# The last map's gate products on two column tiles and its LoRA products on four row tiles of TensorE

## The chip, the cores and the metric

The kernel runs on one core of a Trainium2 chip. The metric is device time in microseconds (us), the median of several executions. One further execution was recorded by the profiler; all durations below come from that one.

## The reference, cut to what matters

The program is a two-layer decoder on two batch rows of 512 tokens and 1024 features, all in float32: a quantized product with the context, a linear map with LoRA, a cross attention with 32 heads, and a last map with LoRA. The change is in the last map (with one small part in the first linear map, which shares a helper). The last map is:

```python
def _L1_ffn_ref(x, W_up, gate_w, expert_bias, lora_A, lora_B):
    x_flat = x.reshape(-1, H)                                  # H = 1024, E = 4 experts, R = 8
    logits = x_flat @ gate_w.T + expert_bias
    top1 = jnp.argmax(logits, axis=-1)
    one_hot = jax.nn.one_hot(top1, E, dtype=x_flat.dtype)
    base_out = jnp.einsum('bth,oh->bto', x, W_up)
    z = jnp.einsum('nh,erh->ner', x_flat, lora_A)
    d = jnp.einsum('ner,ehr->neh', z, lora_B) * SCALE          # SCALE = 1
    delta = jnp.einsum('neh,ne->nh', d, one_hot)
    return base_out + delta.reshape(B, T, H)
...
x = x + _L1_ffn_ref(_layernorm(x, axis=-1), L1_ffn_W_up, L1_ffn_gate_w, L1_ffn_expert_bias, L1_ffn_lora_A, L1_ffn_lora_B)
```

So each token needs 36 numbers from its normalized row (4 logits and 4 x 8 values of z), keeps the 8 values of the expert with the largest logit, and adds a rank-32 product of them to its output row.

## The kernel before

**Stages.** In order of time: keys and values of both batch rows with the quantized product beside them, the first linear map (about 470 to 600 us of the span), the queries, 64 attention heads (two batch rows of 32) until about 2380 us, and the last map, woven into the end of the attention for batch row 0 and alone for batch row 1. Rows 0 to 3 of a batch row are its four tiles of 128 tokens; `rows(b, t)` is tile t.

**The big products.** Every 512 x 1024 x 1024 map is done as seven half-size products instead of eight (a Strassen-like scheme), by `seven_onto` (L304). A map is two blocks s = 0, 1, called a and b here; each does its products in the order 1, 2, 6, 7, 5, 4, 3. Each product is four matmuls over the contraction into one PSUM bank (`accumulate`, L345), taken by VectorE (L320, L317; ScalarE at L315 for product 1) into the rows. Products 1 and 6 give a common sum u, and GpSimd adds u to the outputs of products 5, 4 and 3, each time after VectorE has added that product (L322). `pair` (L325) interleaves them as a1 b1 a2 b2, then a's other five, then b's other five.

**The LoRA products before.** In `linear` (L562), products 2, 4, 5 and 3 of each block take a fifth matmul (L575 to L577): `tT()` holds the selected z of the tokens, transposed, with 32 used rows padded to 128, as halves of the tokens and their difference (`split_tokens`, L585), and `bl` is lora_B, padded to 128 rows. So one map has 8 LoRA matmuls.

**The gate before.** `gated` (L939) is a generator. Four steps multiply, for each tile t of 128 tokens, the normalized rows (as weights, 128 x 128) with the 36 gate and LoRA-A columns `ga_t` (as the moving operand) over 8 chunks of the contraction, into one wide PSUM tile (L946). A step on VectorE then selects the expert, tile by tile (L958 to L970, seven small instructions for each), into z, whose unused columns GpSimd has set to zero (L968). The last step transposes the four z on TensorE (L980), copies them out (L981) and takes the difference of the halves.

**Order.** TensorE runs its instructions in the order in which they are written, in the whole kernel. From the start of the attention's loop to the end of head 63's softmax, VectorE, ScalarE and GpSimd do so too; outside of it their order is a planner's. `hooks` (from L1174) hang pieces of the last map of batch row 0 onto phases of the attention's loop. After phase 1 of iteration 62 come the four gate steps (L1188), after phase 2 of that iteration the selection (L1189), after phase 1 of iteration 63 the transposes of z (L1207) and products a1 and b1 (L1213). In phase 2 of iteration 62, GpSimd gets the four sums of head 63's softmax (L801 to L806), and ScalarE the copy of that head's maximum (L791) and its exponentials (L798), which VectorE prepares (L795). Once the attention's loop has given the rest of its projection, products a4 to b3 of batch row 0 are woven with the layer norm, transposes (L204; copied out by ScalarE, L205, and VectorE, L206) and gate of batch row 1 by `turned_and_gated` (L1227); then the map of batch row 1 runs alone (L1247 to L1251), and its four rows are written out (L1253).

**Buffers.** PSUM has two wide buffers of two banks (`ps_wide`) and four of one bank (`ps_b`, and `ps_tr` of the same kind).

Of the kernel before, what the change touches and what calls it, by code (L numbers as in the profile page):

```python
# [39 lines left out]
def decoder_kernel(  # L40
# [263 lines left out]
    def seven_onto(product, place, order=(1, 6, 2, 7, 5, 4, 3)):  # L304

        banks = {}
        for i in order:
            first = {2: 1, 4: 7, 3: 5}.get(i, i)
            if i == first:
                banks[i] = ps_b()  # L310
            acc = banks[first]
            product(i, acc, i == first)
            if i == 1:
                u = u2([P, HALF])
                nc.scalar.copy(u, acc)  # L315
            elif i == 6:
                nc.vector.tensor_tensor(u, u, acc, ALU.add)  # L317
            else:
                c = place(*{2: (0, 0), 7: (1, 1), 5: (1, 1), 4: (1, 0), 3: (0, 1)}[i])
                nc.vector.tensor_tensor(c, c, acc, ALU.add)  # L320
                if i != 2 and i != 7:
                    nc.gpsimd.tensor_tensor(c, c, u, ALU.add)  # L322
            yield
# [238 lines left out]
    def linear(b, h_ops, w_ops, tT, bl):  # L562

        def blocks(s):
            lora = {2: (0, 0), 4: (1, 0), 5: (1, 1), 3: (2, 1)}

            def product(i, acc, start):
# [12 lines left out]
                (1, 2, 6, 7, 5, 4, 3),  # L580
            )
# [357 lines left out]
    def gated(quarters):  # L939


        zT, diff = u2([P, S]), u2([P, 256])
        gaccs = ps_wide().rearrange("p (t n) -> p t n", t=NT)
        for t in range(NT):
            for c in range(NC):
                nc.tensor.matmul(  # L946
                    gaccs[:, t, :NGA],
                    chunk(quarters, c, t),
                    ga_t[:, c, :],
                    start=(c == 0),  # L950
                    stop=(c == NC - 1),
                )
            yield
        zs = []
        for t in range(NT):
            gacc = gaccs[:, t, :]
            lg = small([P, E1])
            nc.vector.tensor_tensor(lg, gacc[:, :E1], eb_t, ALU.add)  # L958
            mx = small([P, 1])
            nc.vector.tensor_reduce(mx, lg, AX.X, ALU.max)  # L960

            nc.vector.tensor_scalar(lg, lg, mx, None, ALU.is_equal)
            nc.vector.tensor_tensor(lg, lg, prefer, ALU.mult)
            nc.vector.tensor_reduce(mx, lg, AX.X, ALU.max)
            nc.vector.tensor_scalar(lg, lg, mx, None, ALU.is_equal)
            if t % 2 == 0:
                z2 = u2([P, 2, P])
                nc.gpsimd.memset(z2, 0.0)  # L968
            z = z2[:, t % 2]
            nc.vector.tensor_tensor(  # L970
                z[:, : E1 * R1].rearrange("p (e r) -> p e r", r=R1),
                gacc[:, E1:NGA].rearrange("p (e r) -> p e r", r=R1),
                lg.unsqueeze(2).to_broadcast([P, E1, R1]),
                ALU.mult,
            )
            zs.append(z)
        yield
        tr = ps_tr()
        for t, z in enumerate(zs):
            nc.tensor.transpose(tr[:, t, :], z, ident)  # L980
        nc.vector.tensor_copy(zT, tr.rearrange("p t n -> p (t n)"))  # L981
        yield split_tokens(zT, diff)
# [193 lines left out]
    for i in range(2):  # L1176
# [11 lines left out]
    hooks[(62, 1)] = [lambda: advance(last["gates"], 4)]  # L1188
    hooks[(62, 2)] = [  # L1189
        lambda: next(last["gates"]),  # L1190
# [3 lines left out]
    with tc.manual_schedule(  # L1194
# [6 lines left out]
        for i in range(3 * (B * NH + 2)):  # L1201
# [4 lines left out]
            if (n - 2, phase) == (63, 1):  # L1206
                zTs = [next(last["gates"]), None]  # L1207
# [3 lines left out]
                nc.sync.dma_start(bl_t, bl1T)  # L1211
                main = linear(0, h_ops, w_ops, lambda: zTs[0], bl_t)
# [9 lines left out]
    for _ in steps:  # L1222
        pass
    hs, norms = normed(1, u4, 4)
    gates = gated(hs)

    def turned_and_gated():  # L1227
        next(norms)
        yield
        next(norms)  # L1230
        yield
        for _ in range(3):
# [3 lines left out]
        next(gates)  # L1236
        yield
# [9 lines left out]
    main = linear(1, token_sums(hs, lambda: u4([P, 4, 256])), w_ops, lambda: zTs[1], bl_t)  # L1247
    advance(main, 2)
    zTs[1] = next(gates)
    for _ in main:  # L1250
        pass  # L1251
    for t in range(NT):
        nc.sync.dma_start(out[1, ts(t, P), :], rows(1, t))  # L1253

# [70 lines left out]
```

## Time and profile before

| what | value |
|---|---|
| time, median of 3 executions | 2483.03 us (2481.97 to 2484.73) |
| the profiled execution: its own time | 2484.01 us |
| its span, first to last instruction | 2482.2 us |
| TensorE matmul, busy | 2436.6 us, 98% of the span |
| VectorE, ScalarE, GpSimd busy | 1839.0, 527.7, 1029.8 us |
| mean granted TensorE clock | 0.991 |
| L946 gate products, both batch rows | 128 recorded matmuls, 16.1 us |
| L347 (all products through `accumulate`) | 3648 recorded matmuls, 1410.8 us |

How to read it: a busy TensorE means that a matmul was in flight, not that the array was full. A float32 matmul of the program is recorded as two passes, each with a weight load (PEld) of its own: the 32 calls at L946 for one batch row stand as 64 records. In a timeline, a line has the start, the time from the first start to the last end, the engine with its line and operation, output and inputs with shapes, and how many instructions were merged; in brackets, how long the engine sat idle before it and who ended that. Matmul ends are modelled, so the start of the next group is the safer mark. PEclk is the granted TensorE clock as a share of full speed.

### The profile page before, as it was taken

To read this page: it belongs to the slowest core of one execution; us is meant where nothing else is said; L and a number is where in the kernel's file an instruction comes from. 1 tells how busy PE (TensorE), PEld (TensorE's weight loads), DVE (VectorE), ACT (ScalarE), POOL (GpSimd) and SP (SyncE) were. 2 spreads that over 40 slices of the span, in tenths; PEclk is the share of its full clock that TensorE was granted. 3 is DMA by queue.
4 is the path that set the end of the run, shared out by engine and by line. 5 is a ranking of instruction groups with operands and counts; after the bars stand their busy time and mean duration, and the time that the engine had idled before them with its cause. 6 is when DMAs were issued, how large, how long until landed. Compare 5 with 4: busy or idle time off the path is not lost.

```text
span 2482.2 us, 19693 instructions
## 1 busy us (share of the span) xinstructions
PE 2436.6 (98%) x6848; PEld 1216.4 (49%) x6856; DVE 1839.0 (74%) x2020; ACT 527.7 (21%) x615; POOL 1029.8 (41%) x552
## 2 busy tenths in 40 slices
PE   7999999999999999999999999999999999999999
PEld 3477458654444443444444444444444444445454
DVE  5848774345886546898888888888898888887552
ACT  1201221011222222322222222222222222222100
POOL 0000010111000002677676767676767576767421
PEclk8999999999999999999999999999999999999999
DMA  7225133013795221343323322542334234324301
GB/s 264 104 88 208 68 122 116 26 60 114 274 335 201 76 97 47 106 128 115 86 79 103 115 84 75 143 148 78 114 110 128 64 98 115 108 70 111 127 26 43
DMA packets 148243, 283.83 MB, mean 114 GB/s; under 512 B 29296, under 2 KB 47232, under 8 KB 146352
## 3 DMA queue, kind: packets, MB, share of 16 engines
q1 hardware_dynamic: 107888, 242.25, 29.0%
q10 hardware_dynamic: 39824, 39.60, 6.5%
q8 instruction: 55, 0.90, 0.1%
q0 software_dynamic: 432, 0.71, 0.1%
q14 instruction: 44, 0.36, 0.0%
HBM read 221.44 MB, written 61.08 MB: 114 GB/s over the span
## 4 chain that ended last, share of the span: by engine, by line
PE 73%; DVE 7%; POOL 2%; issue 2%; DMA 1%; ACT 1%; POOLq 0%; SPq 0%; ACTq 0%; DVEq 0%
PE b L347 38%; PE wide L749 16%; PE b L812 15%; PE wide L713 2%; DVE u L795 1%; PE wide L204 1%; DMA u<-in_wo_dram 1%; PE wide L946 1%; PE b L636 1%; DVE u L763 1%; POOL u L805 1%; DVE u L775 1%; DVE u L773 0%; POOL u L804 0%; DVE u L320 0%
## 5 line engine op out<-in xcount | busy, mean ns | idle before, releaser
L347 PE MATMUL b<-u,u 128*128 128x512 f32 (+1 forms) x3648 | 1410.8, 544 | 23.2 <-DVE u L291 10.2
L347 PEld LDWEIGHTS b<-u,u 128*128 128x128 f32 x3648 | 692.4, 191 | 706.8 <-issue 625.1
L812 PE MATMUL b<-u,u 128*128 128x512 f32 x1024 | 463.4, 596 | 0.0
L749 PE MATMUL wide<-u,u 128*128 128x512 f32 x1024 | 455.5, 596 | 7.1 <-DVE u L763 6.2
L763 DVE TENSOR_TENSOR u<-wide,u 128x1024 f32<-128x1024 f32 x256 | 313.0, 1225 | 135.7 <-PE wide L749 134.3
L798 ACT ACTIVATE u<-u 128x2048 f32<-128x2048 f32 x128 | 244.6, 1911 | 654.3 <-DVE u L795 572.3
L749 PEld LDWEIGHTS wide<-u,u 128*128 128x128 f32 x1024 | 194.1, 191 | 257.0 <-issue 178.2
L795 DVE TENSOR_TENSOR u<-u,b 128x2048 f32<-128x2048 f32 x128 | 290.2, 2269 | 0.0
L801 POOL TENSOR_TENSOR u<-u 128x1024 f32<-128x1024 f32 x64 | 151.5, 2367 | 318.8 <-ACT u L798 309.6
L812 PEld LDWEIGHTS b<-u,u 128*128 128x128 f32 x1024 | 187.5, 193 | 186.5 <-issue 186.5
L322 POOL TENSOR_TENSOR u<-u,u 128x512 f32<-128x512 f32 x120 | 189.2, 1597 | 197.5 <-DVE u L320 177.9
L320 DVE TENSOR_TENSOR u<-u,b 128x512 f32<-128x512 f32 x200 | 135.8, 680 | 135.4 <-PE b L347 135.3
L222 POOL TENSOR_TENSOR u<-u,sin_t 128x512 f32<-128x512 f32 x8 | 11.7, 1457 | 387.2 <-ACT u L217 387.2
L804 POOL TENSOR_TENSOR u<-u,u 128x1024 f32<-128x1024 f32 x64 | 150.6, 2354 | 36.1 <-ACT u L798 35.7
L805 POOL TENSOR_TENSOR u<-u,u 128x1024 f32<-128x1024 f32 x64 | 151.6, 2369 | 5.0
L823 POOL TENSOR_TENSOR u<-u,u 128x512 f32<-128x512 f32 x64 | 117.8, 1841 | 21.8 <-DMA u<-row 21.8
L1062 POOL DMA_DIRECT2D u<-in_b_dram x1 | 0.6, 558 | 303.5 <-DVE u L245 303.5
L216 ACT ACTIVATE u<-u 64x512 f32<-64x512 f32 x72 | 45.2, 628 | 350.1 <-DVE u L293 168.5
L713 PEld LDWEIGHTS wide<-ident,u 128*128 128x128 f32 x512 | 80.1, 204 | 65.8 <-issue 54.6
L771 DVE TENSOR_TENSOR u<-u 128x1024 f32<-128x1024 f32 x64 | 110.9, 1732 | 0.0
L773 DVE TENSOR_TENSOR u<-u,u 128x1024 f32<-128x1024 f32 x64 | 105.2, 1644 | 0.2
L806 POOL TENSOR_TENSOR u<-u 128x512 f32<-128x512 f32 x64 | 100.5, 1570 | 5.0
(127 smaller groups left out, 1648.3 us busy)
## 6 DMA issues: line engine op xcount, KB each, us to landing
u<-row ACTq DMA_DIRECT2D x128, 256.0 KB, 3.7
u<-wo SPq DMA_DIRECT2D x64, 512.0 KB, 4.2
u<-in_wo_dram SPq DMA_DIRECT2D x48, 512.0 KB, 4.5
u<-in_wq_dram SPq DMA_DIRECT2D x32, 512.0 KB, 4.0
q<-u SPq DMA_DIRECT2D x64, 256.0 KB, 2.4
u<-in_wo_dram SPq DMA_DIRECT2D x16, 1024.0 KB, 7.9
wo<-u SPq DMA_DIRECT2D x32, 512.0 KB, 4.7
u<-q SPq DMA_DIRECT2D x64, 256.0 KB, 4.5
```

The source lines that it names most:

```text
L320: nc.vector.tensor_tensor(c, c, acc, ALU.add)
L322: nc.gpsimd.tensor_tensor(c, c, u, ALU.add)
L347: nc.tensor.matmul(acc, lhsT, rhs, start=start and k == 0, stop=k == len(pairs) - 1, skip_group_check=True,)
L713: nc.tensor.transpose(tr[:, t, :], src[:, t, :], ident)
L749: nc.tensor.matmul(sc[:, ts(n, HALF)], self.kT[:, ts(2 * j + n, P)], self.qT, start=True, stop=True,)
L763: nc.vector.tensor_tensor(self.e[j // 2][:, js, :], sc.rearrange("p (k q) -> p k q", k=2), mask[j], ALU.add)
L795: nc.vector.tensor_tensor(e, e, self.nmf.unsqueeze(1).to_broadcast([P, 4, S]), ALU.add)
L798: nc.scalar.activation(e, e, AF.Exp)
L801: nc.gpsimd.tensor_tensor(d, e[:, 0:2, :], e[:, 2:4, :], ALU.add)
L804: nc.gpsimd.tensor_tensor(d, d, e[:, 0:2, :], ALU.add)
L805: nc.gpsimd.tensor_tensor(d, d, e[:, 2:4, :], ALU.add)
L812: nc.tensor.matmul(self.acc, self.v[:, k, :], self.e[j][:, k % 4, :], start=(k == 0), stop=(k == NKT - 1),)
```

## The change

The gate products of `gated` swap their operands. The 36 columns become the weights and the normalized rows move past them, 256 tokens at a time. Even chunks of the contraction go to the column tile of the array whose results land in PSUM partitions 0 to 35, odd chunks to the one for partitions 64 to 99, so two partial sums arise. ScalarE copies them into a tile `sums` that GpSimd has zeroed, TensorE transposes `sums` back to tokens in rows, and VectorE adds the two partial sums. The selection is done in one set of instructions for all four token tiles, and z is written four times, side by side, so that after its transpose every group of 32 partitions holds a copy.

The LoRA products leave `linear`. The new `add_lora` does them with a contraction of 32 on four row tiles, four matmuls for each pair of token tiles, each into a bank of its own, and VectorE adds the results to the rows. It is called once for each batch row: for row 0 after the attention's last projection, for row 1 after product b2. `bl_t` is loaded as four copies of the 32 used rows.

`seven_onto` gets an option that `linear` uses for both linear maps: GpSimd adds u to the three outputs as soon as product 6 has completed it. Finally, in the output of batch row 1, tile 1 is written last, in two halves.

```diff
--- before.py
+++ after.py
@@ -301,9 +301,14 @@
                 emit(0, 1, u)
             yield
 
-    def seven_onto(product, place, order=(1, 6, 2, 7, 5, 4, 3)):
+    def seven_onto(product, place, order=(1, 6, 2, 7, 5, 4, 3), u_first=False):
 
         banks = {}
+        places = {2: (0, 0), 7: (1, 1), 5: (1, 1), 4: (1, 0), 3: (0, 1)}
+
+        def add(c, what):
+            nc.gpsimd.tensor_tensor(c, c, what, ALU.add)
+
         for i in order:
             first = {2: 1, 4: 7, 3: 5}.get(i, i)
             if i == first:
@@ -315,11 +320,14 @@
                 nc.scalar.copy(u, acc)
             elif i == 6:
                 nc.vector.tensor_tensor(u, u, acc, ALU.add)
+                if u_first:
+                    for k in (5, 4, 3):
+                        add(place(*places[k]), u)
             else:
-                c = place(*{2: (0, 0), 7: (1, 1), 5: (1, 1), 4: (1, 0), 3: (0, 1)}[i])
+                c = place(*places[i])
                 nc.vector.tensor_tensor(c, c, acc, ALU.add)
-                if i != 2 and i != 7:
-                    nc.gpsimd.tensor_tensor(c, c, u, ALU.add)
+                if i != 2 and i != 7 and not u_first:
+                    add(c, u)
             yield
 
     def pair(a, b):
@@ -562,7 +570,7 @@
     def linear(b, h_ops, w_ops, tT, bl):
 
         def blocks(s):
-            lora = {2: (0, 0), 4: (1, 0), 5: (1, 1), 3: (2, 1)}
+            lora = {} if tT is None else {2: (0, 0), 4: (1, 0), 5: (1, 1), 3: (2, 1)}
 
             def product(i, acc, start):
                 pairs = [
@@ -578,6 +586,7 @@
                 product,
                 lambda i, j: rows(b, 2 * i + s)[:, ts(j, HALF)],
                 (1, 2, 6, 7, 5, 4, 3),
+                True,
             )
 
         return pair(blocks(0), blocks(1))
@@ -939,47 +948,71 @@
     def gated(quarters):
 
 
-        zT, diff = u2([P, S]), u2([P, 256])
-        gaccs = ps_wide().rearrange("p (t n) -> p t n", t=NT)
-        for t in range(NT):
+        zT = u2([P, S])
+        z = u2([P, NT, P])
+
+        acc, sums = ps_b(), u2([P, S])
+        nc.gpsimd.memset(sums, 0.0)
+        parts = [slice(64 * i, 64 * i + NGA) for i in range(2)]
+        for th in range(2):
             for c in range(NC):
                 nc.tensor.matmul(
-                    gaccs[:, t, :NGA],
-                    chunk(quarters, c, t),
+                    acc[parts[c % 2], ts(th, 256)],
                     ga_t[:, c, :],
-                    start=(c == 0),
-                    stop=(c == NC - 1),
+                    quarters[th][c // 4][:, c % 4, :],
+                    start=(c < 2),
+                    stop=(c >= NC - 2),
                 )
-            yield
-        zs = []
+            for part in parts:
+                nc.scalar.copy(sums[part, ts(th, 256)], acc[part, ts(th, 256)])
+            yield
+        tr, both = ps_tr(), u2([P, NT, NGA])
         for t in range(NT):
-            gacc = gaccs[:, t, :]
-            lg = small([P, E1])
-            nc.vector.tensor_tensor(lg, gacc[:, :E1], eb_t, ALU.add)
-            mx = small([P, 1])
-            nc.vector.tensor_reduce(mx, lg, AX.X, ALU.max)
-
-            nc.vector.tensor_scalar(lg, lg, mx, None, ALU.is_equal)
-            nc.vector.tensor_tensor(lg, lg, prefer, ALU.mult)
-            nc.vector.tensor_reduce(mx, lg, AX.X, ALU.max)
-            nc.vector.tensor_scalar(lg, lg, mx, None, ALU.is_equal)
-            if t % 2 == 0:
-                z2 = u2([P, 2, P])
-                nc.gpsimd.memset(z2, 0.0)
-            z = z2[:, t % 2]
+            nc.tensor.transpose(tr[:, t, :], sums[:, ts(t, P)], ident)
+        nc.vector.tensor_copy(both, tr[:, :, parts[0]])
+        nc.vector.tensor_tensor(both, both, tr[:, :, parts[1]], ALU.add)
+        lg = small([P, NT, E1])
+        by_expert = lambda t: t.unsqueeze(1).to_broadcast([P, NT, E1])
+        nc.vector.tensor_tensor(lg, both[:, :, :E1], by_expert(eb_t), ALU.add)
+        mx = small([P, NT])
+        by_token = mx.unsqueeze(2).to_broadcast([P, NT, E1])
+        nc.vector.tensor_reduce(mx, lg, AX.X, ALU.max)
+
+        nc.vector.tensor_tensor(lg, lg, by_token, ALU.is_equal)
+        nc.vector.tensor_tensor(lg, lg, by_expert(prefer), ALU.mult)
+        nc.vector.tensor_reduce(mx, lg, AX.X, ALU.max)
+        nc.vector.tensor_tensor(lg, lg, by_token, ALU.is_equal)
+        for k in range(4):
             nc.vector.tensor_tensor(
-                z[:, : E1 * R1].rearrange("p (e r) -> p e r", r=R1),
-                gacc[:, E1:NGA].rearrange("p (e r) -> p e r", r=R1),
-                lg.unsqueeze(2).to_broadcast([P, E1, R1]),
+                z[:, :, ts(k, E1 * R1)].rearrange("p t (e r) -> p t e r", r=R1),
+                both[:, :, E1:].rearrange("p t (e r) -> p t e r", r=R1),
+                lg.unsqueeze(3).to_broadcast([P, NT, E1, R1]),
                 ALU.mult,
             )
-            zs.append(z)
         yield
         tr = ps_tr()
-        for t, z in enumerate(zs):
-            nc.tensor.transpose(tr[:, t, :], z, ident)
+        for t in range(NT):
+            nc.tensor.transpose(tr[:, t, :], z[:, t, :], ident)
         nc.vector.tensor_copy(zT, tr.rearrange("p t n -> p (t n)"))
-        yield split_tokens(zT, diff)
+        yield zT
+
+    def add_lora(b, zT, bl):
+
+        K = E1 * R1
+        for i in range(2):
+            accs = [ps_wide() for _ in range(2)]
+            for k in range(4):
+                j, nh = k // 2, k % 2
+                nc.tensor.matmul(
+                    accs[j][:, ts(nh, HALF)],
+                    zT[ts(k, K), ts(2 * i + j, P)],
+                    bl[ts(k, K), ts(nh, HALF)],
+                    start=True,
+                    stop=True,
+                )
+            for j in range(2):
+                xs = rows(b, 2 * i + j)
+                nc.vector.tensor_tensor(xs, xs, accs[j], ALU.add)
 
 
     ctx.enter_context(tc.manual_schedule(engines={mybir.EngineType.PE}))
@@ -1185,9 +1218,8 @@
         fetch_rows,
         begin_map,
     ]
-    hooks[(62, 1)] = [lambda: advance(last["gates"], 4)]
+    hooks[(62, 1)] = [lambda: advance(last["gates"], 3)]
     hooks[(62, 2)] = [
-        lambda: next(last["gates"]),
         lambda: fetch_weight(7, 0, 1),
         lambda: fetch_weight(3, 1, 1),
     ]
@@ -1204,12 +1236,13 @@
             for act in hooks.get((n - 2, phase), ()):
                 act()
             if (n - 2, phase) == (63, 1):
-                zTs = [next(last["gates"]), None]
+                zT = next(last["gates"])
                 h_ops, parts = last["h"], last["w"]
                 w_ops = lambda i, c: parts[i - 1][:, c, :]
                 bl_t = u4([P, D])
-                nc.sync.dma_start(bl_t, bl1T)
-                main = linear(0, h_ops, w_ops, lambda: zTs[0], bl_t)
+                for k in range(4):
+                    nc.sync.dma_start(bl_t[ts(k, E1 * R1), :], bl1T[: E1 * R1, :])
+                main = linear(0, h_ops, w_ops, None, None)
                 advance(main, 2)
 
     h_ops[:] = token_sums(last["hs"], lambda: u4([P, 4, 256]))
@@ -1221,20 +1254,19 @@
     advance(main, 5)
     for _ in steps:
         pass
+    add_lora(0, zT, bl_t)
     hs, norms = normed(1, u4, 4)
     gates = gated(hs)
 
     def turned_and_gated():
         next(norms)
         yield
-        next(norms)
-        yield
-        for _ in range(3):
+        for _ in range(2):
+            next(norms)
+            yield
             next(norms)
             next(gates)
             yield
-        next(gates)
-        yield
         next(gates)
         yield
 
@@ -1244,13 +1276,18 @@
         pass
     for t in range(NT):
         nc.sync.dma_start(out[0, ts(t, P), :], rows(0, t))
-    main = linear(1, token_sums(hs, lambda: u4([P, 4, 256])), w_ops, lambda: zTs[1], bl_t)
+    main = linear(1, token_sums(hs, lambda: u4([P, 4, 256])), w_ops, None, None)
     advance(main, 2)
-    zTs[1] = next(gates)
+    zT = next(gates)
+    advance(main, 2)
+    add_lora(1, zT, bl_t)
     for _ in main:
         pass
-    for t in range(NT):
+
+    for t in (0, 2, 3):
         nc.sync.dma_start(out[1, ts(t, P), :], rows(1, t))
+    for i in range(2):
+        nc.sync.dma_start(out[1, ts(1, P), ts(i, HALF)], rows(1, 1)[:, ts(i, HALF)])
 
 
 def rope_tables():
```

## The prediction, made before the changed kernel was run

> **What bounds the kernel now.** I read the page's busy times first, then TensorE's timeline from 2240 us to the end, then the other engines at each gap in it. TensorE is busy 98% of the span, and in the first linear map every stretch of 10 us shows it busy for 10.00, so what counts is TensorE's time and the few places where it waits. This is TensorE alone around the gate of batch row 0, and then its last group:
>
> ```profile
> 2278.36 7.03 PE L347 MATMUL b<-u,u 128*128 128x512 f32 x16
> 2285.23 8.61 PE L946 MATMUL wide<-ga_t,u 128*128 128x36 f32 x64
> 2293.65 1.09 PE L713 MATMUL wide<-ident,u 128*128 128x128 f32 x4
> 2294.53 8.58 PE L812 MATMUL b<-u,u 128*128 128x512 f32 x16
> 2302.95 5.31 PE L347 MATMUL b<-u,u 128*128 128x512 f32 x12
> 2308.96 0.33 PE L980 MATMUL b<-ident,u 128*128 128x128 f32 x1 [0.70 <-DVE u L970]
> 2311.12 0.36 PE L980 MATMUL b<-ident,u 128*128 128x128 f32 x1 [1.83 <-DVE u L970]
> 2313.99 0.47 PE L980 MATMUL b<-ident,u 128*128 128x128 f32 x1 [0.93 <-DVE u L970]
> 2314.25 8.96 PE L347 MATMUL b<-u,u 128*128 128x512 f32 x16
> 2323.05 0.63 PE L713 MATMUL wide<-ident,u 128*128 128x128 f32 x4
> ...
> 2428.41 48.23 PE L347 MATMUL b<-u,u 128*128 128x512 f32 x112
> ```
>
> Sixteen passes of 512 columns take 6.87 us from start to start (2278.36 to 2285.23), 0.429 each. Sixteen at L812 took 8.42, and sixteen at L347 after the transposes 8.80. The windows by microsecond say why:
>
> ```profile
> 2291.00:2292.00 1.00, 1.00 (x7) 1.00 (x6) 0.00 (x0) 0.00 (x0) 1.00 (x2) 0.50 0.00 0
> 2312.00:2313.00 1.00, 0.42 (x1) 0.18 (x1) 0.82 (x5) 0.00 (x0) 0.00 (x0) 0.50 0.98 397
> ```
>
> After the window and the five engines, the last three numbers are clock, DMA share and GB/s: the clock halves twice, from about 2291 to 2297.3 in and after the gate products, and from 2311.7 to 2317.9 in and after the waits for z. Those waits come from VectorE's selection, which waits for GpSimd's zeroing:
>
> ```profile
> 2289.17 3.72 POOL L322 TENSOR_TENSOR u<-u,u 128x512 f32<-128x512 f32 x3
> 2299.88 2.36 POOL L801 TENSOR_TENSOR u<-u 128x1024 f32<-128x1024 f32 x1 [6.99 <-ACT u L798]
> 2308.37 0.56 POOL L968 MEMSET u<- 128x256 f32 x2
> ```
>
> The end is one product, VectorE's add, GpSimd's add and a DMA:
>
> ```profile
> 2476.68 0.69 DVE L320 TENSOR_TENSOR u<-u,b 128x512 f32<-128x512 f32 x1 [3.61 <-PE b L347]
> 2477.44 1.26 POOL L322 TENSOR_TENSOR u<-u,u 128x512 f32<-128x512 f32 x1 [3.03 <-DVE u L320]
> ```
>
> [...]idle from about 2308.3, half speed from 2311.7, full again 3.7 us after dense work began at 2314.25. [...] No tiled matmul is in this trace. [...]
>
> **1. Gate of batch row 0.** The old path, from L946 at 2285.2 to the transposes of head 63's sum (L713) at 2323.1, is 37.9 us. Now the new one. A pass of 256 columns takes 0.215 us (L636: 32 passes from 528.78 to 535.69). One half of the tokens is 8 matmuls, 16 passes, 3.43 us on one tile. If the two passes of one matmul follow each other on one tile, and passes start in order, the second pass of one tile can lie beside the first of the next: 8.5 slots, 1.83 us. Bounds: 1.72 (full overlap) to 3.43 (none). So the first half ends at 2287.0.
>
> Then ScalarE's copies need `sums` zeroed. That memset stands on GpSimd behind the three adds of the fence, which end at 2292.9; at twice 128x256 (0.31 us alone, 0.56 for two) it takes 0.5: 2293.4. Two copies of 36x256 follow. ScalarE takes 0.59 for 512 columns and 0.29 for one, hence 0.44 each: 2294.35. [...]TensorE waits until then, idle for 7.3 us and down to half clock: 3.4 us instead of 1.8, to 2297.8; two more copies, 2298.75; four transposes at 0.11, 2299.2. I assume that the clock is back then. Queued behind on TensorE are L713 (0.47) and L812 (6.87): 2306.6, where before they ended at 2302.95. So the first part loses 3.6 us.
>
> But z is then ready early. VectorE's selection is 12 instructions, two of 144 elements (0.25), six of 16 (0.16), four of 128 (0.3), with gaps 3.0 us in all: 2302.2. So the transposes of z at 2311.7 (after L347, 5.15) take 0.44 without a wait, the next 16 passes 6.87, and L713 stands at 2319.1 instead of 2323.1: **4.0 us won**. Behind the selection on VectorE stand L715, L786 and both L795; behind the copies on ScalarE L791. I followed them: VectorE's adds from 2303.2, exponentials until 2309.7, GpSimd's four sums until 2315.9. L713 of head 63 needs these, and 2315.9 is 3.2 us before 2319.1, so this cover holds; it is gone if GpSimd comes 3.2 us later. Bounds: no bank wait gives 6.2; no overlap of column tiles 2.4; a clock that doesn't recover in the second half takes another 2.1. I take 3.5.
>
> **2. LoRA of batch row 0.** Removed: 8 matmuls, 16 passes of 0.429, 6.86 us. Added: two groups of four row tiles. Each group is 8 passes; in order with one slot shared it takes 5 slots, 2.15 us[...]. VectorE's adds are 128x1024 out of PSUM, 1.23 us (L763's row). The second group needs the wide buffers that these adds free: the path is half a group, two adds, half a group. Here VectorE still has the last sum of weights (L267, 2.46, started at 2379.51 when a buffer came free) and two L320 ahead, so the first add begins about 2.1 us after the projection's end, the second group can use its buffers 3.3 and 4.6 after it, and ends at 5.9. In the old run TensorE stood 0.84 us here, waiting for L267; that is now covered. Net 6.86 - 5.9 + 0.84 = **1.8 won**; bounds 0.8 to 2.3.
>
> **3. Gate of batch row 1.** Removed: four groups of 16 passes at 0.107, 1.71 each, 6.84 us. Added: two halves of 1.83. Each now stands right behind the transposes of its own second token tile, which the old order had out of the way, and these copies take:
>
> ```profile
> 2396.10 0.59 ACT L205 COPY u<-wide 128x512 f32<-128x512 f32 x1 [3.72 <-PE wide L204]
> 2396.71 0.69 DVE L206 COPY u<-wide 128x512 f32<-128x512 f32 x1 [0.80 <-ACT u L205]
> ```
>
> The first four chunks need ScalarE's copy, so TensorE waits 0.65 in each half; VectorE's lands beside these four. Four transposes more, 0.44. Sum 2 x 2.48 + 0.44 = 5.4: **1.4 won**; without overlap 8.6, 1.8 lost. Memset and copies have 3.4 us of products beside them: nothing.
>
> **4. LoRA of batch row 1.** 6.86 removed. VectorE has one L320 (0.69) before: half a group 1.29, two adds 2.46, half a group 1.29, with handovers 5.2. **1.7 won**; bounds 0 to 2.6.
>
> **5. The end.** GpSimd's last add and its handover leave the path, 1.33 us. The last DMA is 256 KB instead of 512; the page has 2.4 us to landing for 256 KB (q) against 2.6 here, 0.2. **1.5 won**; bounds 1.2 to 1.9.
>
> **6. Mode changes.** About ten entries and exits. [...]a lone transpose with its latency is 0.33, so 0 to 0.33 each. I take 0.1: **1.0 lost**.
>
> **At nothing.** GpSimd's earlier adds in both linear maps: u is complete at product 6, the first add takes 1.26, and VectorE needs that output 3.43 later. The three extra DMA issues for `bl_t` (0.46 each on SP) delay wo loads that are used some 45 us later; the bytes are the same.
>
> Sum: 3.5 + 1.8 + 1.4 + 1.7 + 1.5 - 1.0 = 8.9. The profiled execution's own time is 2484.0 (span 2482.2 and 1.8 around it), so 2475.1; it stood 1.0 above the median, so **2474.0 us** for the median, 0.4% less.
>
> **The rivals.** **A: more overlap.** The second half doesn't wait for the copies, or all passes of different tiles lie side by side: 6.2 + 2.3 + 1.6 + 2.6 + 1.5 - 0.5 = 13.7, 2469. [...] **B: the tiles don't overlap** in float32: 2.4 + 0.8 - 1.8 + 0 + 1.5 - 1.0 = 1.9, 2481. What remains is the shorter end and the covered selection. **C: tiles that don't overlap[...].** There are some 24 changes for each batch row (16 in the gate, 8 in LoRA), 48 in all, in place of the 1.0. At half of a lone transpose, 0.165, they cost 7.9: 2.9 - 7.9, 5.0 lost, 2488. It decides for slower from 0.06 us a change. [...]
>
> **How the numbers follow.** Forecast 0.55 (2470.5 to 2478), A 0.22, B 0.18, C 0.05. A measurement of this kernel can tell 0.2%, 5 us, from no change, so faster is below 2478.1. That holds nearly all of the forecast, A, and a little of B: 0.77; same 0.18; slower 0.05. The range, 2468 to 2481, takes A's middle and B's, and leaves out C and the ends.
>
> **What would show it.** Gate: TensorE idle about 7 us between the halves, with half clock, and the memset at 2293; L980 without waits; L713 near 2319. LoRA: two groups with a wait for VectorE of about 0.5 to 1.3 in between. Starts in the tiled groups closer than a pass show overlap. End: no GpSimd after the last add. I am wrong if the passes don't overlap, if the clock stays low through L812, or if L713 of head 63 waits for GpSimd.

## The result, and the profile after

| what | before | after |
|---|---|---|
| time, median of 12 executions each | 2483.22 us (2480.85 to 2485.35) | 2475.72 us (2473.65 to 2482.5) |
| ratio after to before | | 0.9976, 95% interval 0.9968 to 0.9983 |
| the profiled execution: its own time | 2484.01 us | 2474.27 us |
| its span, and its mean granted clock | 2482.2 us, 0.991 | 2472.5 us, 0.992 |

The changed kernel is faster by 0.24%, about 6 us (4.2 to 7.9 by the interval). The forecast of 2474.0 was 1.7 us too low and its range holds the result; its gain of 9 us lies just outside the interval.

The two profiled executions differ by 9.7 us, but 4.3 of these lie ahead of the first changed instruction of the gate (it starts at 2285.23 before, at 2280.96 after), in stretches with the same instructions on TensorE. In the eight kernels below that have the changed kernel's TensorE code up to there, the gate starts anywhere from 2280.28 to 2285.60. So I count this part as chance and compare stage by stage from there:

| stretch of TensorE | before | after | won | forecast |
|---|---|---|---|---|
| gate of row 0 to the transposes of head 63's sum | 37.82 | 34.26 | 3.56 | 3.5 |
| from there to the first transposes of row 1 (L204) | 67.66 | 73.05 | -5.39 | -0.8 |
| from there to the transposes of z of row 1 | 37.26 | 33.57 | 3.69 | 4.0 |
| from there to the last matmul's end | 48.67 | 46.63 | 2.04 | 1.7 |
| from there to the span's end | 5.56 | 4.03 | 1.53 | 1.5 |
| sum | | | 5.43 | 9.9, less 1.0 for mode changes |

(In the forecast's column, the 1.8 of its step 2 is split: three of the eight removed products, 2.57, stood in the third stretch, so the second should have lost 0.8.) The 5.43 agree with the 6 of the ratio. One stretch is wrong, the second. TensorE's timeline of the kernel after, with its new line numbers (L959 gate, L971 transposes of the sums, L995 transposes of z, L722 and L821 what L713 and L812 were, L1006 the LoRA groups, L355 the products):

```profile
2280.96 1.93 PE L959 MATMUL b<-u,ga_t 128*36 128x256 f32 x16
2289.79 3.64 PE L959 MATMUL b<-u,ga_t 128*36 128x256 f32 x16 [6.91 <-ACT u L967]
...
2307.92 0.60 PE L995 MATMUL b<-ident,u 128*128 128x128 f32 x4
...
2315.22 0.63 PE L722 MATMUL wide<-ident,u 128*128 128x128 f32 x4
...
2370.72 1.14 PE L1006 MATMUL wide<-u,u 32*128 32x512 f32 x8
2373.95 2.08 PE L1006 MATMUL wide<-u,u 32*128 32x512 f32 x4 [2.09 <-DVE u L1015]
2376.65 2.07 PE L1006 MATMUL wide<-u,u 32*128 32x512 f32 x4 [0.61 <-DVE u L1015]
2378.65 9.79 PE L355 MATMUL b<-u,u 128*128 128x512 f32 x16
2388.27 1.03 PE L204 MATMUL wide<-ident,u 128*128 128x128 f32 x8
...
2431.68 2.26 PE L1006 MATMUL wide<-u,u 32*128 32x512 f32 x8 [1.31 <-DVE u L1015]
2433.87 34.60 PE L355 MATMUL b<-u,u 128*128 128x512 f32 x80
```

First the gate. Its 16 passes of 256 columns take 1.93 us, where one column tile takes 3.64 (measured below), so the column tiles overlap; then TensorE stands 6.91 us, the second half runs at half clock (3.64), and z is ready early enough that L995 has no wait. Then the LoRA groups of row 0. Eight passes take 1.14, where 8 x 0.429 = 3.43 is the estimate for one tile, so the row tiles overlap; but the second group waits 2.09 and 0.61, its halves of four passes take 2.08 each, and the 16 passes behind it 9.62 from start to start, not 6.87. Row 1 has the same wait shape, 1.31, and the 80 passes after it at full speed (34.60, 0.43 each). The windows of the kernel after (clock third from the right) show the cause of the 9.62:

```profile
2375.00:2376.00 1.00, 1.00 (x4) 0.00 (x0) 1.00 (x2) 0.00 (x0) 0.00 (x0) 0.50 0.00 0
...
2384.00:2385.00 1.00, 1.00 (x4) 0.52 (x3) 0.00 (x0) 0.00 (x0) 0.00 (x0) 0.99 0.00 0
```

In windows of 0.1 us the half clock lasts from 2373.8 to 2384.0. VectorE's timeline shows why the second group was late:

```profile
2372.69 1.21 DVE L1015 TENSOR_TENSOR u<-u,wide 128x1024 f32<-128x1024 f32 x1
2374.78 0.69 DVE L163 BATCH_NORM_STATS2 small<-u 128x6 f32<-128x512 f32 x1 [0.88 <-POOL u L310]
2375.39 1.20 DVE L1015 TENSOR_TENSOR u<-u,wide 128x1024 f32<-128x1024 f32 x1
```

The first add comes 2.0 us after the projection's end (2370.72), as forecast. Between it and the second stands an instruction of row 1's layer norm (L163), which itself waits 0.88 for GpSimd: TensorE can use the second buffer 5.9 us after the projection's end, 1.3 later than forecast. GpSimd's timeline at the gate, and the last line of the whole timeline:

```profile
2284.80 3.70 POOL L310 TENSOR_TENSOR u<-u,u 128x512 f32<-128x512 f32 x3
2288.43 0.53 POOL L955 MEMSET u<- 128x512 f32 x1
```

```profile
2469.30 0.33 SPq L1290 DMA_DIRECT2D out_dram<-u  x1
```

The zeroing stands behind three adds of the projection, and at the end no GpSimd add is left between VectorE's last add (2468.58 to 2469.27) and the last DMA's issue.

### The profile page after: what moved, and what is told of

Same layout as the page of the kernel before. It is cut to its first block, busy times and chain, and to the rows that moved or that the text cites. A ratio compares the mean times of both kernels' runs of the same rounds, so it can differ in the third digit from the quotient of the medians.

```text
span 2472.5 us, 19595 instructions
## 1 busy us (share of the span) xinstructions
PE 2422.1 (98%) x6800; PEld 1201.3 (49%) x6800; DVE 1839.4 (74%) x1994; ACT 530.4 (21%) x623; POOL 1031.2 (42%) x550
## 4 chain that ended last, share of the span: by engine, by line
PE 74%; DVE 6%; POOL 2%; issue 2%; DMA 1%; ACT 1%; ACTq 0%; SPq 0%; POOLq 0%; DVEq 0%
PE b L355 39%; PE wide L758 16%; PE b L821 15%; PE wide L722 2%; DVE u L804 2%; PE wide L204 1%; POOL u L814 1%; DVE u L772 1%; POOL u L813 1%; PE b L645 1%; DMA u<-in_wo_dram 1%; DVE u L782 1%; DVE u L784 1%; ACT u L807 0%; DVE u L328 0%
## 5 line engine op out<-in xcount | busy, mean ns | idle before, releaser
L355 PE MATMUL b<-u,u 128*128 128x512 f32 (+1 forms) x3616 | 1397.0, 544 | 22.5 <-DVE u L291 10.2
L355 PEld LDWEIGHTS b<-u,u 128*128 128x128 f32 x3616 | 687.2, 191 | 699.0 <-issue 615.8
L821 PE MATMUL b<-u,u 128*128 128x512 f32 x1024 | 460.4, 593 | 0.0
L821 PEld LDWEIGHTS b<-u,u 128*128 128x128 f32 x1024 | 186.4, 192 | 184.4 <-issue 184.4
L722 PEld LDWEIGHTS wide<-ident,u 128*128 128x128 f32 x512 | 80.1, 204 | 65.2 <-issue 55.1
```

Source lines behind the costliest of these rows:

```text
L355: nc.tensor.matmul(acc, lhsT, rhs, start=start and k == 0, stop=k == len(pairs) - 1, skip_group_check=True,)
L821: nc.tensor.matmul(self.acc, self.v[:, k, :], self.e[j][:, k % 4, :], start=(k == 0), stop=(k == NKT - 1),)
```

## The experiments

My theory after the comparison: the tiled products themselves are nearly free; what the change costs is two places in which TensorE waits inside a tiled sequence (the zeroing in the gate, VectorE's adds in the LoRA groups), and the half clock after each. Rivals: row tiles bring the clock down by themselves; the waits only move elsewhere. The first four kernels ran on one chip (before there: 2482.68), the next four on another (2482.62), the last three on a third (2483.74); each is compared by its ratio to the kernel before.

**The three parts alone.** Each kernel is the kernel before with one part of the diff: the gate (with z still padded and the LoRA products still in `linear`); the LoRA groups (with the old gate, z written four times for each token tile); `u_first` and the order of the output. Against the kernel before, beside the lines of the diff that each takes over, the first two have:

```diff
-        yield split_tokens(zT, diff)
+        yield split_tokens(zT, u2([P, 256]))
```

```diff
+            for k in range(4):
+                nc.vector.tensor_tensor(
+                    z[:, ts(k, E1 * R1)].rearrange("p (e r) -> p e r", r=R1),
...
-        yield split_tokens(zT, diff)
+        yield zT
```

and the third only takes over lines:

```diff
+    def seven_onto(product, place, order=(1, 6, 2, 7, 5, 4, 3), u_first=False):
...
+    for t in (0, 2, 3):
```

> The kernel before with the new gate alone (two column tiles, one set of selection); the LoRA products stay inside the seven products and the end stays as before. Theory: the parts add up, so this one is worth what the changed trace shows for it, 3.6 us from the gate of batch row 0 to head 63's sum and 1.1 in the gate of batch row 1: 4.7 us faster, about 2478.5. Rival: what the gate wins is given back later, at the last sum of weights (L267) before product a4 or at head 63's sum, which the other parts hid: then under 2 us, 2481 or more.

Measured: 2477.86 us, ratio 0.9981 (0.9973 to 0.9988), so 4.7 won, and the rival falls. TensorE again stands 6.91 between the halves, and the gate's stretch is again 34.26. The gate does what the forecast says.

> The kernel before with the LoRA part alone: z written four times, add_lora on row tiles, no fifth matmuls; the gate products and the selection tile by tile stay as before. Theory: row 0's add_lora holds TensorE 8.1 us, against 6.9 removed and 0.8 covered, and half clock after it takes up to 2.8 more, while row 1 wins 2.0: between 2.4 us faster and 1 us slower, 2481 to 2484. Rival, the prediction as it stood: 1.8 + 1.7 - 0.4 = 3.1 us faster, 2480, with add_lora of row 0 under 6 us.

Measured: 2485.81 us, ratio 1.0011 (1.0005 to 1.0018), 3 us slower. The rival, a gain of 3, is refuted; the theory's range was too low as well. The profiled execution (2490.44) took 4.6 more than this median, so its trace shows where time goes, not how much goes on average. Its gate stretch is 38.72 instead of 37.82, but the trace doesn't put this down to the four writes of z: TensorE waits 4.1 in all for the transposes of z (4.6 before), while the old gate's products happened to run longer at half clock (10.88 instead of 8.61). The larger losses are in the groups. In the timeline, row 1's group waits the same 1.31 as in the kernel after, but the 80 passes behind it take 37.22, not 34.60:

```profile
2441.57 2.98 PE L992 MATMUL wide<-u,u 32*128 32x512 f32 x8 [1.31 <-DVE u L1001]
2444.49 37.22 PE L347 MATMUL b<-u,u 128*128 128x512 f32 x80
```

By windows of 0.1 us the clock is half from 2443.0 to 2449.8 there, as it is from 2384.9 to 2391.8 after row 0's groups. So the same wait costs 1.3 us in one run and 1.3 + 3.4 in another (0.7 in the second group, 2.6 in the products behind it).

> The kernel before with GpSimd's additions moved ahead in both linear maps and the last rows written in halves; gate and LoRA as before. Theory: only the tail changes, 1.5 us faster, 2481.7, from TensorE's last matmul to the end 4.0 us instead of 5.6. Rival: GpSimd's early additions make VectorE wait in the maps, so that TensorE stands there and the gain is gone: 2483 or more.

Measured: 2483.0 us, ratio 0.9996 (0.9986 to 1.0006): the time can't tell. The trace can: from the start of VectorE's last add to the span's end are 5.52 us before, 4.03 here, 3.92 in the kernel after. The rival has no support in it: in the first linear map (470 to 600 us) TensorE is busy for 130.00 of 130 us, as before. By the ratios the three parts add up to 3 us (4.7 - 2.7 + 1.0), each with an interval of 1.5 to 2.5 us either way, so they neither contradict nor confirm the 6 of the whole.

**The LoRA groups apart.** The kernel after, with each group of four matmuls at a place of its own, products between them:

```diff
-    def add_lora(b, zT, bl):
+    def add_lora(b, zT, bl, i):
...
-    add_lora(0, zT, bl_t)
+    add_lora(0, zT, bl_t, 0)
...
+    next(main)
+    next(side)
+    next(main)
+    add_lora(0, zT, bl_t, 1)
+    next(side)
...
-    add_lora(1, zT, bl_t)
+    add_lora(1, zT, bl_t, 0)
+    advance(main, 2)
+    add_lora(1, zT, bl_t, 1)
```

> The changed kernel with each add_lora cut in two, the second group of four row tiles two products later (after a3, and after a7 of batch row 1), so that TensorE never waits for VectorE to free the wide buffers. Theory: TensorE's waits in add_lora and the half clock that follows them are the loss. Each group then takes about 1.0 us of TensorE, row 0 saves 6 us and up to 2.8 of clock, row 1 saves 2.6: 8.6 to 11 us under the changed kernel, 2465 to 2467, full clock through a4 and a3. Rival: row tiles, which use a quarter of the array's rows, bring the clock down by themselves: then half clock still follows the group, and 6 us or less are won.

Measured: 2472.52 us, ratio 0.9959 (0.9946 to 0.9971), by the ratios 4 better than the kernel after (their intervals overlap slightly; the traces from the gate on give 5.7), not 8.6 or more. TensorE's timeline:

```profile
2376.42 7.13 PE L355 MATMUL b<-u,u 128*128 128x512 f32 x16
...
2387.73 1.57 PE L204 MATMUL wide<-ident,u 128*128 128x128 f32 x8 [3.11 <-DVE u L1014]
2389.09 4.85 PE L355 MATMUL b<-u,u 128*128 128x512 f32 x8
```

No group waits, and the products behind the first run at full clock (7.13): row tiles beside dense work don't bring it down here, and that rival falls. But the second group now sits right before L204, which needs the same two wide buffers: the wait moved there, 3.11, with half clock after it (4.85 for eight passes).

**The zeroing earlier.** The kernel after, with the tile of row 0's sums zeroed one iteration of the attention's loop earlier:

```diff
-        acc, sums = ps_b(), u2([P, S])
-        nc.gpsimd.memset(sums, 0.0)
+        acc = ps_b()
+        sums = sums or zeroed()
...
-        last["gates"] = gated(hs)
+        last["gates"] = gated(hs, last["sums"])
...
+    hooks[(61, 1)] = [lambda: last.update(sums=zeroed())]
```

> The tile of sums of batch row 0 is zeroed one iteration of the attention's loop earlier; all else as in the changed kernel. Theory: the 6.91 us in which TensorE stands between the two gate halves is mostly the wait for that zeroing, which stands behind three adds on GpSimd, and only the rest is the bank that both halves share. So the wait falls to about 0.9 us (the two copies of the first half), the clock stays full, the second half takes 1.8 instead of 3.6, and 6.0 + 1.8 + 1 = 8 to 9 us are won, about 2467. The transposes of head 63's sum then stand at TensorE so early that they may wait for GpSimd by 0 to 2 us. Rival: GpSimd's four sums of head 63 are late by nearly all of what is won, the wait only moves to those transposes and little is gained: at most 4 us, 2471.5 or more.

Measured: 2473.26 us, ratio 0.9956 (0.9943 to 0.9969). The theory's mechanism is there, 6.91 became 0.89 at full clock, but by the ratios only 5 us are won over the kernel after (4.0 by the traces from the gate on), near the rival's 4 and far from 8 to 9. TensorE's timeline, and ScalarE's:

```profile
2283.10 1.92 PE L964 MATMUL b<-u,ga_t 128*36 128x256 f32 x16 [0.89 <-ACT u L972]
...
2299.99 3.06 PE L355 MATMUL b<-u,u 128*128 128x512 f32 x4 [2.90 <-ACT u L320]
```

```profile
2290.70 0.33 ACTq L731 DMA_DIRECT2D row<-small  x1
...
2296.56 0.33 ACTq L737 DMA_DIRECT2D u<-row  x1
2296.93 1.91 ACT L807 ACTIVATE u<-u 128x2048 f32<-128x2048 f32 x1 [2.15 <-DMA row<-small]
...
2299.34 0.59 ACT L320 COPY u<-b 128x512 f32<-128x512 f32 x1
```

The new wait isn't where the rival had it. TensorE waits for a PSUM bank that ScalarE's copy L320 empties; the copy stands behind head 63's exponentials, and these behind a row of 2 KB that ScalarE writes out (L731) and reads back (L737). That row takes 5.8 us to land, 2.7 in the kernel after. Here a fetch of 1 MB is issued 0.41 us ahead of it, there 0.45 behind it.

**Both.** Early zeroing, the two gate halves in two banks of one wide tile, and the groups apart (row 0's second one now before b's product 3). The first four lines are against the early zeroing alone, the rest against the kernel after:

```diff
-        acc = ps_b()
+        acc = ps_wide()
...
-                    acc[parts[c % 2], ts(th, 256)],
+                    acc[parts[c % 2], HALF * th : HALF * th + 256],
...
-    weave(main, side, 1)
+    for k in range(7):
+        if k == 6:
+            add_lora(0, zT, bl_t, 1)
+        next(main)
+        next(side, None)
```

> Early zeroing, the two gate halves in two banks, and the LoRA groups apart: group 1 of batch row 0 at the end of the projection, group 2 before b's product 3, group 2 of batch row 1 after a's product 7. Theory: the waits and the half clocks after them are what the tiled products cost, so without them 8 to 9 us (gate) and 8 to 10 us (LoRA, since the first transposes of batch row 1 no longer wait for a wide buffer) come off the changed kernel: 2457 to 2461, with no clock below 0.95 for more than 2 us after 2280. Rival: the second group before b's product 3 meets the layer norm's work on VectorE and the wait moves to a bank of a product there; then it gives no more than the early zeroing alone and the split alone together less 3 us, 2463 or more.

Measured: 2462.11 us, ratio 0.9911 (0.9898 to 0.9924), between the two expectations. The LoRA part is as the theory has it, TensorE's timeline has no wait from the first group to the gate of row 1, and the 16 passes in between take 6.97 from start to start:

```profile
2370.04 1.14 PE L1010 MATMUL wide<-u,u 32*128 32x512 f32 x8
...
2378.08 1.04 PE L204 MATMUL wide<-ident,u 128*128 128x128 f32 x8
```

From the projection's end to L204 are 8.04 us, 17.55 in the kernel after, where both groups stand in that stretch. The wait for ScalarE's copy stays, 3.07, with half clock from 2301.7 to 2308.5. And the second gate half still waits 0.89 for ScalarE, although it writes another bank.

**One row tile, one column tile.** The kernel after, with all four LoRA matmuls of a group on row tile 0, and with all chunks of the gate on column tile 0.

```diff
-                    zT[ts(k, K), ts(2 * i + j, P)],
-                    bl[ts(k, K), ts(nh, HALF)],
+                    zT[ts(0, K), ts(2 * i + j, P)],
+                    bl[ts(0, K), ts(nh, HALF)],
```

> All four LoRA matmuls of a group on row tile 0 (its copy of z and of the weights), the rest as in the changed kernel; same sizes and same result. Theory: the row tiles run beside each other although each float32 matmul is two passes, which is why 8 passes take 1.07 us from first start to the next group. On one tile they take 8 x 0.429 = 3.4 at full clock, and less waiting for VectorE in between, since VectorE's adds start when the banks are filled: 1.3 to 4.7 us slower than the changed kernel over the two batch rows. Rival: passes of 32 rows are short on any tile, or the groups are bound by VectorE's adds alone: within 1 us of the changed kernel.

Measured: 2486.13 us, ratio 1.0015 (1.0008 to 1.0022), 10 slower than the kernel after: the overlap is real, and both expectations are too small. TensorE's timeline of this run, and one of its windows:

```profile
2372.20 11.35 PE L1006 MATMUL wide<-u,u 32*128 32x512 f32 x16
```

```profile
2375.00:2376.00 1.00, 1.00 (x3) 0.48 (x2) 0.44 (x1) 0.00 (x0) 1.00 (x1) 0.50 0.00 0
```

TensorE never waits, and is busy 1.00 in every window, yet the clock halves 2.7 us after the one-tile products begin; in row 1 again, from 2439.8 to 2446.6.

```diff
-                    acc[parts[c % 2], ts(th, 256)],
+                    acc[parts[0], ts(th, 256)],
...
-                    start=(c < 2),
-                    stop=(c >= NC - 2),
+                    start=(c == 0),
+                    stop=(c == NC - 1),
...
-            for part in parts:
+            for part in parts[:1]:
```

> All eight chunks of a gate half on column tile 0, one partial sum instead of two (the other part of the sums stays zero); the rest as in the changed kernel; same result. Theory: the column tiles run beside each other, 16 passes of 256 columns in 1.8 us, and on one tile take 3.43. In batch row 1 that costs 2 x 1.6 = 3.2 us, less what of it hides ScalarE's and VectorE's copies; in batch row 0 the first half hides in the wait for the zeroing, and the second half, at half clock, costs up to 3.4 more. One copy less on ScalarE gives back 0.35 each. Together 3 to 6 us slower than the changed kernel. Rival: order of issue bounds the passes, not the tile: within 1 us.

Measured: 2482.59 us, ratio 0.9996 (0.9988 to 1.0005), 5 slower than the kernel after by the ratios. A half takes 3.64 on one column tile, and row 1's stretch is 37.01 instead of 33.57. The theory holds. TensorE's timeline of the first half of row 1, and a window inside it:

```profile
2397.90 3.64 PE L959 MATMUL b<-u,ga_t 128*36 128x256 f32 x16 [0.68 <-ACT u L205]
```

```profile
2397.97:2401.38 3.41, 3.41 (x16) 1.66 (x16) 0.60 (x1) 0.00 (x0) 2.90 (x3) 1.00 0.02 5
```

Here 36 of the array's 128 columns are in use for 3.6 us, and the clock over this window is 1.00.

**Two tiles for the halves; the rows later.** First the early zeroing with one PSUM tile for each half (the first piece of code, against the early zeroing alone); then, in two kernels with everything so far, the same, and the same with one 1 MB fetch issued later and on another queue (the second piece, against its companion):

```diff
-        acc = ps_b()
...
         for th in range(2):
+            acc = ps_b()
```

```diff
-        for t, d in zip(x[0], x_d[0]):
-            nc.sync.dma_start(t, d)
+        nc.sync.dma_start(x[0][0], x_d[0][0])
...
     hooks[(62, 2)] = [
+        lambda: nc.scalar.dma_start(x[0][1], x_d[0][1]),
```

> As the early zeroing, with one PSUM tile for each gate half instead of one for both. With both banks in one tile the second half still waited 0.89 us for ScalarE's copies. Theory: the wait belongs to the common tile (the program orders a later write to a tile behind an earlier read of it, whichever bank), so with two tiles it is gone, the two halves follow each other in 1.85, and the transposes of the sums wait about 0.7 for the last copy. The time stays within 1 us of the early zeroing, since TensorE then waits that much longer for ScalarE's copy out of a product's bank, 2.9 becoming 3.8. Rival: the wait is for something else that ScalarE's copies mark (the rows or the zeroed tile), and stays at 0.9.

Measured: 2469.89 us, ratio 0.9945 (0.9932 to 0.9959). The intervals of this and the early zeroing alone overlap, so by time they aren't told apart. TensorE's timeline has the answer:

```profile
2285.62 1.92 PE L964 MATMUL b<-u,ga_t 128*36 128x256 f32 x16 [0.15 <-ACT u L829]
```

The wait for the copies is gone (the 0.15 is another buffer). With two banks in one tile it was there, so it came from the common tile (0.89 with it, 0.15 without), not from the bank. The wait for L320 was 2.62, not 3.8: seen from the gate's start, the row was issued 0.45 us sooner here, and it landed in 5.3 instead of 5.8.

> Both waits gone and two tiles for the gate halves, nothing else: the companion of the next run, which differs from it in one transfer only. Theory: 2462 within 1.5 us, with a wait of 3.5 to 4 us of TensorE for ScalarE's copy behind head 63's exponentials. Rival: the 0.9 us less in the gate comes through, 2460.5 or less.

> As the run before, but the second half of the input rows of batch row 0 (1 MB) is fetched from ScalarE's queue after head 63's exponentials instead of from SyncE's as soon as its buffer is free. Theory: in the runs with early zeroing this fetch starts 0.45 us ahead of the 2 KB row of sums that ScalarE writes out and reads back, so the row takes 5.8 us to land instead of 2.7, and head 63's exponentials and the copy behind them come 3 us late. With the fetch out of the way the row lands in about 3, TensorE's wait for that copy falls from 3.5 or more to about 1, the clock is not halved after it, and 3 to 5 us are won: about 2458. Rival: the weights that stand behind that fetch on SyncE start 3 us earlier in its place and hold up the row just as long; the wait stays above 2.5 us and less than 1.5 us is won.

Measured: 2462.63 us, ratio 0.9914 (0.9901 to 0.9928), and 2458.37 us, ratio 0.9900 (0.9887 to 0.9914), 4.3 apart by the medians (3.5 by the ratios, whose intervals overlap; the stretch of row 0's gate is 29.31 and 26.56, so the traces show 2.75). From the issues of transfers (size, and the median time to landing), first without, then with the fetch moved:

```profile
row<-small ACTq DMA_DIRECT2D x1, 2.0 KB, 5.2
```

```profile
row<-small ACTq DMA_DIRECT2D x1, 2.0 KB, 2.3
```

TensorE's timeline with the fetch moved:

```profile
2299.64 1.98 PE L355 MATMUL b<-u,u 128*128 128x512 f32 x4 [1.72 <-ACT u L320]
```

The row lands in 2.3, the wait is 1.72 instead of 2.92 (expected were about 1 and 3.5 to 4), the gate's 32 passes of row 0 follow each other in 3.65, and every window taken from 2280 to 2449.3 has a clock of 1.00; the 64 passes at the end take 27.73, 0.43 each. This is the fastest version: by the ratios 25 us under the kernel before, 19 under the kernel after. Its gain over the kernel after is 7.7 in the gate's stretch (26.56 us), 9.5 up to L204 (63.54), 2.3 in row 1's products (44.33), less 1.3 for the group that moved into the stretch between; 18 in all.

## Why the prediction was right or wrong

**Term 1, gate of row 0: right**, 3.56 for 3.5, and by its mechanism: the memset behind three adds, the idle of 6.91 (forecast 7.3), the half clock, L995 without a wait. Its reason for the wait was wrong in part: with the zeroing moved 0.89 of the 6.91 remain, and these belong to the program's common tile. The forecast put the wait down to the bank, which no trace of before shows: it was its author's assumption. In the run with two banks of one tile the wait stays (0.89), with two tiles it goes (0.15 is left, for another buffer).

**Term 2, LoRA of row 0: wrong.** It forecast 1.8 won, and the traces show about 3 lost (6.86 removed and 0.84 covered, against 7.93 for the groups and 2.75 of half clock behind them). Two things failed in it. The path of 5.9 took "group, two adds, group" with the adds back to back; VectorE's queue had an instruction of the next layer norm between them. And it put the clock at nothing, without a reason: the 2.75 are not in its sum. The pass model there was wrong in the other direction (a group takes 1.07, not 2.15), but that time was only spent waiting. That the groups are the cost is shown by the LoRA part alone (3 us slower) and by the kernels with the groups apart.

**Term 3, gate of row 1: right**, the waits of 0.68 and 0.67 at ScalarE's copies are the forecast 0.65; 1.1 won for 1.4. **Term 4: right**, 2.04 for 1.7, with a wait of 1.31 in it; that the clock stayed full there was luck: in the LoRA part alone it is half from 2443.0 to 2449.8, behind the same wait. **Term 5: right**, 1.5 for 1.5, in the trace of the end alone too. **Term 6: right in size**: eight passes behind a gate half take 3.54 instead of 3.44, 16 ahead of the gate 6.96 instead of 6.87, and 16 between two LoRA groups 7.06 where these stand apart, so about 0.1 for an exit and 0.1 for an entry.

**The whole.** From the gate on, the traces have 5.4 won for 8.9. Term 2 alone is 4.6 to 4.8 short. The others come out near their forecasts, and the 1.0 for mode changes is already inside the measured stretches. That the total of 2474.0 came within 1.7 us of the median is in part luck.

**Its reading of the clock.** Windows of 1 us misled it by up to 0.4: the clock falls at 2290.8 and 2311.3, not at 2291 and 2311.7. And TensorE is idle ahead of the second fall alone: it is busy for all of the 3.41 us ahead of the first. TensorE also waits 1.10 for a third transpose of z (2312.58), which the forecast does not list.

**The rivals.** A had the overlap of the row tiles right and the time wrong. What it gives the groups, 2.3 and 2.6, comes out within 0.1 if half a group takes two passes of 0.429, 0.86: an estimate, and nothing else in the trace of before speaks for it. B and C fall with the one-tile runs: tiles do overlap in float32. A gate half takes 1.92 on two column tiles and 3.64 on one; two LoRA groups of row 1 take 1.14 each on four row tiles (where they stand apart) and 8.27 together on one, the last 2.4 of that at half clock. As an estimate, the changes of tile inside a group cost at most what 1.07 us is more than two passes of 0.43, 0.2 for all of them.

## What to carry to other kernels

Price a tiled or narrow sequence by the waits inside it and by the clock after it, not by its passes (row 0's groups: 2.70 of waits and 2.75 of half clock, against 1.07 for the passes of one): put it between dense products, in groups small enough that no group waits for the buffers of the one before (apart, groups took 1.07 without a wait). Before you count a following engine's steps as back to back, look at what its queue holds between them (here L163, 0.69 and its wait of 0.88). And when a stage gets shorter, look at which transfers its freed buffers start, and whether a small one on the path comes behind them (the row of 2 KB landed in 5.2 behind the fetch of 1 MB, in 2.3 without it).

## What the runs showed of the hardware

The stretches at half clock last: in the kernel after 10.3 and 10.2 us (2285.0 to 2295.3 and 2373.8 to 2384.0), in the kernel before 6.8 twice (2290.8 to 2297.6, 2311.3 to 2318.1), on one row tile 13.7 (2374.9 to 2388.6) and 6.8 (2439.8 to 2446.6). The falls named are 88.8 apart in the kernel after, 20.5 in the kernel before, 64.9 on one row tile. All of these are whole multiples of about 3.415 us within 0.1 (3, 3, 2, 2, 4, 2; 26, 6, 19); the 3.415 is an estimate from these times alone. Here is what TensorE did in some stretches of 3.41 us, ahead of a fall or where the clock stayed full:

- In the kernel before, TensorE is busy for all 3.41 us up to 2290.8, in the old gate with 36 columns at a time, and the clock halves. In the 3.41 up to the fall at 2311.3 it is busy for 0.88, and two transposes stand between the waits.
- With both waits gone, a stretch with 1.03 us of dense passes and 2.38 idle (up to 2301.7) ends in half clock.
- In the kernel after, behind one with 1.31 idle, 0.8 dense and the rest tiled (up to 2431.8) the clock stays full. In the LoRA part alone, one with 1.31 idle and only tiled work (up to 2443.0) ends in half clock. TensorE is busy for 2.1 us in both.
- On one row tile, two stretches have no idle at all. Behind the one with 0.98 dense and 2.44 on the tile (up to 2436.4) the clock stays full, the one with 0.68 and 2.74 (up to 2374.9) ends in half clock.
- On one column tile, a stretch with nothing but passes over 36 of 128 columns (2397.97 to 2401.38, the seventh behind the fall at 2377.5) has full clock, and so have the products behind it (eight passes in 3.53 from start to start).

So TensorE was busy throughout both in stretches that ended in half clock (up to 2290.8 and 2374.9) and in stretches that didn't (up to 2436.4 and 2401.38), and among the second is one with 36 of the array's 128 columns in use. Busy time alone doesn't tell them apart, and neither does the share of the array that the weights fill (128*128 in the old gate up to 2290.8, 128*36 on the column tile). What does, no run here shows.
